# Output of attention in two half sums on 64x32 tiles, placed as pieces in the two lanes of TensorE

## The chip, the core and the metric

One Trainium2 chip, of which the program uses one core. The metric is the time of one execution of the whole kernel on the device, in microseconds (us). One core has a TensorE (PE, whose weight loads the profile lists apart as PEld), a VectorE (DVE), a ScalarE (ACT), a GpSimd (POOL), a SyncE (SP) that issues most transfers, an on-chip memory of 128 partitions, and eight accumulator banks that TensorE writes.

## What is computed

A diffusion transformer block on 16 samples of 256 tokens by 256 features, with 16 heads of 16 features, all in fp32:

```python
x_norm = modulate(_ln(x), shift_a, scale_a)
q, k, v = jnp.split(x_norm @ W_qkv + b_qkv, 3, axis=-1)
attn_w = softmax(einsum('bhqd,bhkd->bhqk', q, k) * scale)
x = x + gate_a * (einsum('bhqk,bhkd->bhqd', attn_w, v) @ W_proj + b_proj)
k_c, v_c = jnp.split(_ln(context) @ W_kvc + b_kvc, 2, axis=-1)
c_attn_w = softmax(einsum('bhqd,bhsd->bhqs', _ln(x) @ W_qc + b_qc, k_c) * scale)
x = x + einsum('bhqs,bhsd->bhqd', c_attn_w, v_c) @ W_cproj + b_cproj
h = gelu(modulate(_ln(x), shift_m, scale_m) @ W_mlp1 + b_mlp1)
x = x + gate_m * (h @ W_mlp2 + b_mlp2)
```

## The kernel before

**Units and beats.** Each sample has two attentions, self (`s`) and cross (`c`): 32 units, one after the other, then a stage for the MLPs. A unit is eight *beats*, one for each pair of heads. In beat k, TensorE makes the scores of pair k of the current unit, keys by queries (words `t`, into the two banks of the tile `st`), and the scores of the next unit's heads, queries by keys (`s`, into the banks `s0` and `s1`), of which VectorE takes the row maxima (`mx`). ScalarE turns `st` into the weights `pt` with one exp of 128x1024 (word `E`, function `exp`). The tile `st` exists once, so the next beat's `t` waits until that exp has read it. Of `pt` there are five buffers.

**Two lanes.** Nearly all matmuls have a contraction of 64 rows. The lower rows (0 to 63) and the upper rows of the array are two lanes that run at the same time. `PLAN` (L1108) has a row for each beat: words issued before, words of lane x (the lower half), words of lane y (the upper half), and words issued after. The function `beside` writes the two lanes into one program order: it always takes the next matmul from the lane whose cost so far is lower. A matmul of 64 rows by 256 columns costs 1, and a transpose of 64 columns costs 0.53 (`HALF`). `Q12` means twelve matmuls of the query projection of a later unit; K, V and P (output projection) likewise. `T`, `U`, `A0`, `A1`, `a`, `m0`, `m1` are transposes by halves (`half_turns`): each half of the array writes its own half of one bank, and the later half first waits (`after`) until the earlier one is complete. All engines execute in the order of the program.

**Output of attention.** `av_part(u, g)` sums weights times values for four heads over all 128 key rows: weights loaded 128x32, so that four heads stand in four strips of 32 columns of the array, and a second pass over the other 128 keys. The words `o0` and `o1` run two such calls each, 16 matmuls in one block that uses the whole array: `o0` behind beat 4 (pairs 0 to 3), `o1` behind beat 0 of the next unit (pairs 4 to 7). fp32 operands take two passes, so the trace has 32 records for these 16 matmuls. ACT then copies the bank (`o`) into `oT`, 128x512. The transposes `A0` and `A1` turn `oT`, `norm` divides by the sums, `a` turns the result back, and P projects it.

**Banks.** Banks 0 and 1 are `st`, 2 and 3 are `s0` and `s1`. The tag `tr` (`SHORT`) has two banks, which the tiles of `T`, `U`, `A0`, `A1`, `a`, `m0`, `m1` and `o` take in turn, and `gen` (`LONG`) two for the projections. A tile that takes a bank waits until the last reader of the tile before has finished.

**Words of ScalarE.** `kh` and `qh` write the high parts of K and Q (two instructions each), `m0s` and `m1s` the negated maxima, `pe` copies the projection (`t_s`, `t_c`), `Te`, `Ue`, `ae` copy transposes (`y_c` or `y_s`, `y_q`, `y_ac`), `Vk` the values (`v`).

Every instruction is issued through one helper, so the profile puts all of them on L51; they are told apart by the names of their tiles.

## Time and profile before

| | |
|---|---|
| time, median of 2 runs | 738.29 us (736.37 to 740.21) |
| profiled execution, its own time | 737.4 us |
| its span, first to last instruction | 735.6 us |
| TensorE busy | 728.9 us (99%) |
| VectorE, ScalarE, GpSimd busy | 584.8, 555.5, 546.3 us |
| blocks of attention output, first to last start | 45.2 to 552.9 us |
| granted TensorE clock | 0.999 |

A row of a timeline reads: start and length in us, engine, line, operation, output tile <- input tiles, shape, count, and in brackets the idle time before it with what ended it. Matmul records are pipelined: each record's length holds the time until its last result is written, so records overlap, and the pace is read from the starts. A row of a group reads: engine, operation, tiles, shapes, count | busy time in us, mean ns of one | idle time before.

### The profile page before, as it was taken

What the parts mean: (1) busy time and instruction counts of PE and PEld (TensorE: products, weight loads), DVE (VectorE), ACT (ScalarE), POOL (GpSimd) and SP (SyncE); (2) the same over time, 40 slices, a digit from 0 to 9 for tenths busy, and PEclk for the clock granted to TensorE, in tenths of its full rate; (3) what the DMA queues carried; (4) which work ended last, traced back from release to release, by engine and by line L of the source; (5) the groups of instructions that cost most, each with busy time, mean ns of one, the idle gap of its engine ahead of it and who ended that gap; (6) DMA issues with size and microseconds to landing.
All of it is one profiled execution on the core that took longest, in us unless ns stands there. A gap on an engine that the chain in (4) does not pass through costs nothing.

```text
span 735.6 us, 25307 instructions
## 1 busy us (share of the span) xinstructions
PE 728.9 (99%) x10112; PEld 644.8 (88%) x10112; DVE 584.8 (79%) x1217; ACT 555.5 (76%) x959; POOL 546.3 (74%) x571
## 2 busy tenths in 40 slices
PE   9999999999999999999999999999999999999997
PEld 9878888888888888888888888888889999999997
DVE  4788898989888888988888989888735577687772
ACT  3268898888888888888888888899887655555553
POOL 6777688869687786968778798788657766767753
PEclk9999999999999999999999999999999999999999
DMA  6754454543545454454545555455312323323331
GB/s 190 205 166 142 125 142 134 141 122 101 155 114 155 125 144 137 107 152 112 160 126 139 143 156 146 126 151 140 96 60 58 102 61 98 98 90 102 87 77 38
DMA packets 94825, 90.60 MB, mean 123 GB/s; under 512 B 9266, under 2 KB 90452, under 8 KB 94708
## 3 DMA queue, kind: packets, MB, share of 16 engines
q1 hardware_dynamic: 94244, 88.20, 42.8%
q8 instruction: 80, 1.31, 0.8%
q0 software_dynamic: 192, 0.52, 0.3%
q14 instruction: 37, 0.30, 0.1%
q10 hardware_dynamic: 272, 0.26, 0.1%
HBM read 26.97 MB, written 8.46 MB: 48 GB/s over the span
## 4 chain that ended last, share of the span: by engine, by line
PE 93%; DVE 3%; POOL 2%; issue 1%; ACT 1%; DMA 1%; SPq 0%; POOLq 0%; ACTq 0%
PE s L51 18%; PE o L51 16%; PE st L51 16%; PE ph L51 10%; PE ps_q L51 5%; PE ps_qc L51 4%; PE ps_v_c L51 3%; PE ps_kc L51 3%; PE ps_P_s L51 3%; PE ps_k L51 2%; PE ps_v_s L51 2%; PE ps_P_c L51 2%; DVE mx L51 1%; PE psT_q L51 1%; PE ps_h L51 1%; PE psA_s L51 1%
## 5 line engine op out<-in xcount | busy, mean ns | idle before, releaser
L51 DVE TENSOR_REDUCE mx<-s 128x2 f32<-128x512 f32 x504 | 324.8, 684 | 64.4 <-PE s L51 57.7
L51 ACT ACTIVATE pt<-st 128x1024 f32<-128x1024 f32 x252 | 258.9, 1027 | 16.4 <-PE st L51 10.4
L51 PE MATMUL s<-big 63*128 63x256 f32 (+1 forms) x1024 | 184.0, 297 | 0.2
L51 PEld LDWEIGHTS s<-big 63*128 63x128 f32 (+1 forms) x1024 | 133.4, 186 | 18.7 <-DVE l_kc L51 6.6
L51 PE MATMUL st<-big 64*128 64x256 f32 (+1 forms) x1024 | 134.6, 298 | 0.5 <-ACT pt L51 0.2
L51 POOL TENSOR_TENSOR hl<-hf,hh 128x512 fp32r<-128x512 f32 x64 | 87.0, 1361 | 52.9 <-ACT hh L51 52.8
L51 PE MATMUL o<-pt,v 128*32 128x256 f32 x2048 | 123.8, 382 | 0.0
L51 PEld LDWEIGHTS st<-big 64*128 64x128 f32 (+1 forms) x1024 | 96.3, 186 | 16.1 <-issue 13.1
L51 PEld LDWEIGHTS o<-pt,v 128*32 128x32 f32 x2048 | 60.1, 110 | 41.4
L51 ACT ACTIVATE hf<-ph,bT 128x256 f32<-128x256 f32 x114 | 47.8, 471 | 33.1 <-PE ph L51 33.0
L51 ACT ACTIVATE hh<-ph,bT 128x256 fp32r<-128x256 f32 x114 | 47.9, 472 | 28.0 <-PE s L51 14.4
L51 ACT COPY oT<-o 128x512 f32<-128x512 f32 x63 | 36.9, 586 | 33.1 <-PE o L51 33.1
L51 PE MATMUL st<-big,hh 128*128 128x256 f32 x256 | 46.7, 282 | 0.0
L51 PE MATMUL s<-big,hh 128*128 128x256 f32 x256 | 46.7, 281 | 0.0
L51 PE MATMUL ph<-wkch,wself 128*128 128x256 f32 x224 | 44.4, 282 | 0.0
L51 PE MATMUL ph<-wqch,wself 128*128 128x256 f32 x224 | 44.3, 282 | 0.0
L51 PE MATMUL ps_k<-xTh_s,wself 64*128 64x256 f32 (+1 forms) x232 | 43.6, 294 | 0.0
L51 POOL TENSOR_SCALAR xn_c<-c,mv_c,rs_c 128x256 f32<-128x256 f32 x32 | 39.0, 1227 | 1.7
L51 PE MATMUL ps_q<-xTh_s,wself 64*128 64x256 f32 (+1 forms) x240 | 39.7, 282 | 0.0
L51 PE MATMUL ps_P_s<-wself,xTh_as 64*128 64x256 f32 x256 | 39.1, 282 | 0.0
L51 PEld LDWEIGHTS s<-big,hh 128*128 128x128 f32 x256 | 39.0, 189 | 0.0
L51 PEld LDWEIGHTS st<-big,hh 128*128 128x128 f32 x256 | 39.0, 189 | 0.0
(250 smaller groups left out, 2500.4 us busy)
## 6 DMA issues: line engine op xcount, KB each, us to landing
big<-h_kc SPq DMA_DIRECT2D x64, 128.0 KB
big<-h_qc SPq DMA_DIRECT2D x64, 128.0 KB
big<-h_k SPq DMA_DIRECT2D x62, 128.0 KB
big<-h_q SPq DMA_DIRECT2D x62, 128.0 KB
big<-l_k SPq DMA_DIRECT2D x32, 128.0 KB
big<-l_q SPq DMA_DIRECT2D x32, 128.0 KB
g<-gd SPq DMA_DIRECT2D x16, 256.0 KB
c<-in_ctx_dram SPq DMA_DIRECT2D x16, 256.0 KB
```

What stands on the lines that cost most here:

```text
L51: i = f(*a, **k)
```

## The change

The sum over 128 key rows is made in two halves of 64 rows. The function `av_halves(u, i)` handles two pairs of heads, 2i and 2i+1, in one bank: half 0 is eight matmuls of 64 rows by 32 columns in the lower half of the array (two blocks of keys times four strips), half 1 eight in the upper half, which add into the same bank and wait for the last matmul of half 0 (`after`). Each half is a word of one lane, `O0` to `O3`, with a cost of 0.91 for a matmul (`OCOST`). `PLAN` now has O0 in beat 3, O1 in beat 5, O2 in beat 7 and O3 in beat 1 of the next unit; the words `o0` and `o1` are gone, and pieces of Q, P and V stand in other beats. `a`, `ae` and `ac` move from beat 5 to beat 4. The copies of `o` become four of 128x256 (`k0` to `k3`, function `av_keep`), each in the words behind its beat. As the heads of a bank are others than before, `norm` writes other columns of `A`, and the rows of W_proj and W_cproj, which are split into high and low parts early on, are loaded a second time in that order by four transfers each (`f_rows`). The last O3 of the program is done whole (`av_all`).

TensorE, from the end of beat 0 of unit 9 (`psm_1` is its `m1`), before: the block `o_2` of unit 8, of which the first four of 16 rows are shown, stands between this beat and the next.

```order
L51 MATMUL st<-big_75 128x256 x2
L51 MATMUL s_111<-big_76 128x256
L51 MATMUL st<-big_75 128x256
L51 MATMUL s_111<-big_76 128x256
L51 MATMUL psm_1_3786<-ident,mx_81 128x64
L51 MATMUL o_2_3808<-pt_4_3618,v_80 32x256
L51 MATMUL o_2_3808<-pt_5_3663,v_80 32x256
L51 MATMUL o_2_3808<-pt_6_3728,v_80 32x256
L51 MATMUL o_2_3808<-pt_7_3773,v_80 32x256
```

The same place in the changed program:

```order
L51 MATMUL s_111<-big_76 128x256
L51 MATMUL st<-big_75 128x256
L51 MATMUL s_111<-big_76 128x256
L51 MATMUL psm_1_4156<-ident,mx_81 128x64
L51 MATMUL s_110<-big_76 128x256
L51 MATMUL st<-big_75 128x256
L51 MATMUL s_110<-big_76 128x256
L51 MATMUL st<-big_75 128x256 x2
L51 MATMUL ps_P_s_4115<-wself,xTh_as_3989 128x256
L51 MATMUL st<-big_75 128x256
L51 MATMUL ps_P_s_4115<-wself,xTh_as_3989 128x256
L51 MATMUL o_3_4192<-pt_6_4078,v_80 32x256
```

Beat 1's `s` and `st` now follow beat 0's directly, and the output of attention comes behind them, one row in turn with the other lane.

TensorE at the start of beat 3 of unit 9 in the changed program (`psT_c` is the word T, `psA_c` A1, `o_0` is O0, whose bank is that of T):

```order
L51 MATMUL psT_c_4251<-ident,xn_c_3891 128x64 x2
L51 MATMUL psA_c_4258<-ident,oT_2_4150 128x64 x4
L51 MATMUL ps_v_s_4275<-wself,xTh_s_3881 128x256 x3
L51 MATMUL s_110<-big_76 128x256
L51 MATMUL ps_q_4210<-xTh_s_3881,wself 128x256
L51 MATMUL s_110<-big_76 128x256
L51 MATMUL ps_q_4210<-xTh_s_3881,wself 128x256
L51 MATMUL o_0_4293<-pt_0_4176,v_78 32x256
L51 MATMUL ps_q_4210<-xTh_s_3881,wself 128x256
L51 MATMUL o_0_4293<-pt_1_4231,v_78 32x256
L51 MATMUL ps_q_4210<-xTh_s_3881,wself 128x256
```

Before, no `o` stood between T and the end of beat 4; now O0 comes a few matmuls behind T.

ScalarE from beat 7 of unit 8 to beat 4 of unit 9, before:

```order
L51 ACTIVATE h_k_3782<-ps_k_3667,bqkv 128x256 x2
L51 ACTIVATE m_1_3799<-psm_1_3786 16x128
L51 ACTIVATE pt_0_3806<-st 128x1024
L51 COPY oT_3_3825<-o_2_3808 128x512
L51 ACTIVATE pt_1_3871<-st 128x1024
L51 COPY t_s_3892<-ps_P_s_3747 128x512
L51 ACTIVATE pt_2_3915<-st 128x1024
L51 COPY y_c_3917<-psT_c_3883 128x512
L51 ACTIVATE pt_3_3949<-st 128x1024
L51 ACTIVATE h_q_3954<-ps_q_3841,bqkv 128x256 x2
L51 ACTIVATE pt_4_3972<-st 128x1024
```

And in the changed program:

```order
L51 COPY oT_2_4150<-o_2_4097 128x256
L51 ACTIVATE h_k_4152<-ps_k_4029,bqkv 128x256 x2
L51 ACTIVATE m_1_4169<-psm_1_4156 16x128
L51 ACTIVATE pt_0_4176<-st 128x1024
L51 ACTIVATE pt_1_4231<-st 128x1024
L51 COPY oT_2_4150<-o_3_4192 128x256
L51 COPY t_s_4268<-ps_P_s_4115 128x512
L51 ACTIVATE pt_2_4279<-st 128x1024
L51 COPY y_c_4281<-psT_c_4251 128x512
L51 ACTIVATE pt_3_4337<-st 128x1024
L51 COPY oT_0_4342<-o_0_4293 128x256
L51 ACTIVATE h_q_4344<-ps_q_4210,bqkv 128x256 x2
```

The copies of `o` now stand ahead of `h_k` and `h_q`, which stand ahead of the exps of beats 0 and 4.

```diff
@@ -255,7 +255,19 @@
 
     def f_split(i):
         w = (Wp, Wkc, Wqc, Wvc, Wcp)[i]
-        split(w[0], w[1], (gA, cB, cB, cB, cB)[i][(3, 2, 3, 4, 1)[i]])
+        if i in (0, 4):
+            f_rows(i // 4)
+        split(w[0], w[1], turned[i] if i in turned else cB[(0, 2, 3, 4)[i]])
+
+    turned = {}
+
+    def f_rows(i):
+        w_ap = (W_proj, W_cproj)[i]
+        t = turned[4 * i] = work.tile([P, KC, H], F32, tag="x1", name=f"wrow{i}", bufs=7)
+        src = w_ap.rearrange("(a k g r) c -> k g a r c", a=2, k=2, g=2)
+        for k in range(KC):
+            for g in range(2):
+                SP.dma_start(t[64 * g:64 * g + 64, k], src[k, g])
 
     wm = []
 
@@ -630,12 +642,11 @@
         def norm(hf):
             if hf == 0:
                 o.A = work.tile([P, NT, H], F32, tag="A", name=f"A_{name}", bufs=1)
-            pv = o.ps.rearrange("p (x h c) -> p x h c", x=4, h=4)
-            rc = work.tile([P, 4, 4, 1], F32, tag="rc", name=f"rc{hf}_{name}")
+            pv = o.ps.rearrange("p (t g c) -> p t g c", t=NT, g=8)
+            rc = work.tile([P, NT, 8, 1], F32, tag="rc", name=f"rc{hf}_{name}")
             DVE.reciprocal(rc, pv[:, :, :, HD:HD + 1])
-            A = o.A.rearrange("p t (r f) -> p (t r) f", r=2)[:, :, 64 * hf:64 * hf + 64]
-            DVE.tensor_tensor(A.rearrange("p x (h i) -> p x h i", h=4),
-                              pv[:, :, :, 0:HD], rc.to_broadcast([P, 4, 4, HD]), ALU.mult)
+            A = o.A[:, :, P * hf:P * hf + P].rearrange("p t (g i) -> p t g i", g=8)
+            DVE.tensor_tensor(A, pv[:, :, :, 0:HD], rc.to_broadcast([P, NT, 8, HD]), ALU.mult)
 
         aT = transposed(lambda: o.A, f"a{name}", pool=True)
 
@@ -766,22 +777,41 @@
             for f in pieces:
                 next(f)
 
-    def av_part(u, g):
-
-        if g % 2 == 0:
-            u.po = ps_gen(f"o_{u.n}_{g}", SHORT).rearrange("p (g n) -> p g n", g=2)
-        for c in range(NT):
-            for h in range(4):
-                par, pair = g % 2, g // 2 * 4 + h
-                PE.matmul(u.po[h * 32:(h + 1) * 32, g % 2], u.v[:, c, par * 8 + pair], u.pt[pair][:, par, c],
-                          start=(c == 0), stop=(c == NT - 1), tile_position=(0, h * 32))
-        if g % 2 == 1:
-            oT = work.tile([P, 2, N], F32, tag="oT", name=f"oT_{u.n}_{g}")
-            last = u.n == nu - 1 and g == 3
-            (DVE.tensor_copy if last else ACT.copy)(oT.rearrange("p g n -> p (g n)"),
-                                                    u.po.rearrange("p g n -> p (g n)"))
-            u.oT.append(oT)
-
+    def av_halves(u, i):
+
+
+        po = ps_gen(f"o_{u.n}_{i}", SHORT)
+        done = []
+
+        def half(hf):
+            rows = slice(64 * hf, 64 * hf + 64)
+            if hf:
+                after(done[0])
+            for c in range(NT):
+                for j in range(4):
+                    par, pair = j // 2, 2 * i + j % 2
+                    ins = PE.matmul(po[32 * j:32 * j + 32, :N], u.v[rows, c, par * 8 + pair], u.pt[pair][rows, par, c],
+                                    start=(hf == c == 0), stop=(hf == 1 and c == NT - 1),
+                                    tile_position=(64 * hf, 32 * j), skip_group_check=True)
+                    if c == NT - 1 and j == 3:
+                        done.append(ins.ins.name)
+                    yield OCOST
+        u.po[i] = po
+        return half(0), half(1)
+
+    def av_keep(u, i):
+        if i % 2 == 0:
+            u.oT.append(work.tile([P, 2, N], F32, tag="oT", name=f"oT_{u.n}_{i}"))
+        last = u.n == nu - 1 and i == 3
+        (DVE.tensor_copy if last else ACT.copy)(u.oT[i // 2][:, i % 2], u.po[i][:, :N])
+
+    def av_all(u, i):
+        for h in av_halves(u, i):
+            for _ in h:
+                pass
+        av_keep(u, i)
+
+    OCOST = 0.91
 
     seq = [("s", b) for b in range(5)]
     for b in range(B):
@@ -794,7 +824,7 @@
         u.n, u.kind, u.b = n, kind, b
         u.qk, u.v = big[n % 3], vts[n % 3]
         u.q, u.k = u.qk[:, 0], u.qk[:, 1]
-        u.oT, u.pt = [], {}
+        u.oT, u.pt, u.po = [], {}, {}
         units.append(u)
     nu = len(units)
 
@@ -1106,14 +1136,14 @@
 
     none = (), ()
     PLAN = [
-        ("kh", "s t m1", "m1 t s", "m1s kH E o1 add gate kl"),
-        ("c1", "s t Q12", "t P2 s P10", "L1 ld kL E"),
-        ("", "s t T pe A1 V3", "s t Q4 T A1 Q1", "hadd E L2 Te Tc c2"),
-        ("", "s t V9", "Q1 t s Q6", "E n1"),
-        ("qh store", "s t", "s t qH", "E L3 o0 ql qL"),
-        ("", "t s a E m0 K6", "t s V4 a m0 V2", "ae ac m0s e5 lc s1"),
-        ("", "s t K1 A0 K5 U E", "V2 t s V4 U A0", "begin e6 Vk Ue s6"),
-        ("", "s t P12", "K2 t s K1 K9", "E n0 Uc s7 e7"),
+        ("kh", "s t m1", "m1 t s", "m1s kH E add gate kl"),
+        ("c1", "s t O3 Q6", "t P2 s P7 O3", "L1 ld kL E k3"),
+        ("", "s t Q6 T pe A1 V3", "s t P3 T A1", "hadd E L2 Te Tc c2"),
+        ("", "s O0 t V9", "Q5 t s Q7 O0", "E n1 k0"),
+        ("qh store", "s t a", "s t V3 qH a", "E L3 ql ae ac qL"),
+        ("", "s O1 t E m0 K6", "t s V4 m0 V2 O1", "m0s k1 e5 lc s1"),
+        ("", "s t A0 K6 U E", "s t V3 U A0", "begin e6 Vk Ue s6"),
+        ("", "s t O2 P12", "K2 t s K1 K9 O2", "E n0 Uc s7 e7 k2"),
     ]
     lanes = {}
 
@@ -1139,15 +1169,10 @@
         c5 = unit(n + 5)
         ln = lambda v, i: lambda *a: v.ln[i].steps
 
-        def attention(v, hf):
-            if v:
-                av_part(v, 2 * hf)
-                av_part(v, 2 * hf + 1)
-
         on = lambda v, f: f if v else lambda: None
         T1 = lx and (lx.T[1],)
         do = {
-            "E": exps, "o1": lambda: attention(prev, 1), "o0": lambda: attention(cur, 0),
+            "E": exps, "k3": on(prev, lambda: av_keep(prev, 3)), **{f"k{i}": lambda i=i: av_keep(cur, i) for i in range(3)},
             "kh": on(q2, lambda: q2.K.high()), "kl": on(q2, lambda: q2.K.low()),
             "kH": on(q2, lambda: q2.K.send_high()), "kL": on(q2, lambda: q2.K.send_low()),
             "qh": on(q2 and hasattr(q2, "Q"), lambda: q2.Q.high()), "ql": on(q2 and hasattr(q2, "Q"), lambda: q2.Q.low()),
@@ -1180,6 +1205,7 @@
             "U": on(lx, lambda: lx.T[1].halves()),
             "A1": on(p1, lambda: p1.halves(1)), "A0": lambda: cur.post.halves(0),
             "a": on(p1, lambda: p1.aT.halves()),
+            "O3": on(prev, lambda: av_halves(prev, 3)), **{f"O{i}": lambda i=i: av_halves(cur, i) for i in range(3)},
         }
         on_x = {"Q": (q2, "Q"), "V": (q2, "V"), "K": (q3, "K"), "P": (None if whole_p else p1, None)}
         on_y = {"Q": (q2, "Q"), "V": (q2, "V"), "K": (q3, "K"), "P": (p2, None)}
@@ -1230,7 +1256,7 @@
     for b in range(2):
         M[b].xT = M[b].src.xT
     done = {
-        "av": lambda: (av_part(last, 2), av_part(last, 3)), "P": lambda: (q.proj(0), q.proj(1)), "PF": q.finish,
+        "av": lambda: av_all(last, 3), "P": lambda: (q.proj(0), q.proj(1)), "PF": q.finish,
         "A1": lambda: o.turn(1), "N1": lambda: o.norm(1), "aT": o.aT.turn, "aL": lambda: (o.aT.high(), o.aT.low_dve()),
         "C": lambda: (o.proj(0), o.proj(1)), "CF": o.finish,
     }
```

## The prediction, made before the result was known

> **What bounds the kernel now.** First the page: its span, the engines, the clock, and the chain that ended last.
>
> ```profile
> span 735.6 us, 25307 instructions
> PE 728.9 (99%) x10112; PEld 644.8 (88%) x10112; DVE 584.8 (79%) x1217; ACT 555.5 (76%) x959; POOL 546.3 (74%) x571
> PEclk9999999999999999999999999999999999999999
> PE 93%; DVE 3%; POOL 2%; issue 1%; ACT 1%; DMA 1%; SPq 0%; POOLq 0%; ACTq 0%
> ```
>
> TensorE carries 93% of the chain at full clock. But a busy PE is not PE at its pace, so next come the starts on TensorE in the timeline around one unit (beat 0 starts at 311.05).
>
> ```profile
> 303.14 0.51 PE L51 MATMUL st<-big 64*128 64x256 f32 x4
> 303.58 1.93 PE L51 MATMUL o<-pt,v 128*32 128x256 f32 x32
> 305.45 0.51 PE L51 MATMUL st<-big 64*128 64x256 f32 x4
> ...
> 310.81 0.28 PE L51 MATMUL ps_P_s<-wself,xTl_as 64*128 64x256 f32 x1
> 310.83 0.28 PE L51 MATMUL ps_k<-xTl_s,wself 64*128 64x256 f32 x1
> 310.93 0.28 PE L51 MATMUL ps_P_s<-wself,xTl_as 64*128 64x256 f32 x1
> 310.95 0.28 PE L51 MATMUL ps_k<-xTl_s,wself 64*128 64x256 f32 x1
> 311.05 0.28 PE L51 MATMUL s<-big 63*128 63x256 f32 x1
> ...
> 311.74 1.94 PE L51 MATMUL o<-pt,v 128*32 128x256 f32 x32
> 313.61 0.39 PE L51 MATMUL st<-big 64*128 64x256 f32 x1
> ...
> 317.29 0.28 PE L51 MATMUL ps_q<-xTh_s,wself 64*128 64x256 f32 x1
> 317.45 0.51 PE L51 MATMUL st<-big 64*128 64x256 f32 x4
> ...
> 319.64 1.94 PE L51 MATMUL o<-pt,v 128*32 128x256 f32 x32
> ```
>
> Both lanes start a matmul every 0.12 us (310.81 to 310.93, 310.83 to 310.95): a step is 0.12. A unit takes 319.64 - 303.58 = 16.06. A block of output lasts 1.87 from its start to the next `st` (303.58 to 305.45). Now ScalarE over the same unit:
>
> ```profile
> 311.27 0.84 ACT L51 ACTIVATE h_k<-ps_k,bqkv 128x256 fp32r<-128x256 f32 x2 [0.54 <-PE ps_k L51]
> 312.13 0.27 ACT L51 ACTIVATE m<-psm 16x128 fp32r<-16x128 f32 x1
> 312.43 1.03 ACT L51 ACTIVATE pt<-st 128x1024 f32<-128x1024 f32 x1
> 313.74 0.59 ACT L51 COPY oT<-o 128x512 f32<-128x512 f32 x1 [0.29 <-PE o L51]
> 314.39 1.02 ACT L51 ACTIVATE pt<-st 128x1024 f32<-128x1024 f32 x1
> 315.88 0.59 ACT L51 COPY t_s<-ps_P_s 128x512 f32<-128x512 f32 x1 [0.47 <-PE ps_P_s L51]
> 316.37 1.03 ACT L51 ACTIVATE pt<-st 128x1024 f32<-128x1024 f32 x1
> 317.28 0.59 ACT L51 COPY y_c<-psT_c 128x512 f32<-128x512 f32 x1
> 318.06 1.02 ACT L51 ACTIVATE pt<-st 128x1024 f32<-128x1024 f32 x1 [0.18 <-PE st L51]
> 318.98 0.83 ACT L51 ACTIVATE h_q<-ps_q,bqkv 128x256 fp32r<-128x256 f32 x2
> 319.81 1.02 ACT L51 ACTIVATE pt<-st 128x1024 f32<-128x1024 f32 x1
> ...
> 324.88 0.58 ACT L51 COPY v<-ps_v_s 128x512 f32<-128x512 f32 x1
> 325.52 0.59 ACT L51 COPY y_q<-psT_q 128x512 f32<-128x512 f32 x1
> ```
>
> The reader is to see a second loop that is nearly as long as TensorE's. `st` starts, 0.6 later the exp (303.14's `st` and 317.45's: 318.06), 1.03 later it ends, and only then may the next `st` start: 1.7 a beat, 8 x 1.7 = 13.6 a unit, without what ScalarE puts in between. In beat 0 the exp starts 1.38 after the beat (312.43 - 311.05), since `h_k` and `m` stand ahead of it, and ends at 313.46. The next `st` starts at 313.61. TensorE doesn't stand still in between, because the block of 311.74 lies exactly there. The block behind beat 4 covers `h_q` and the exp of 319.81 in the same way. **The two blocks are TensorE's work and the cover of the exp loop at once.** That a waiting `st` holds both lanes shows at 317.29 to 317.45: the exp of 316.37 ends at 317.40, and although V and Q steps stand behind `st` in both lanes, nothing starts before it.
>
> **The change, part by part.** First the groups of like instructions that give the length of a single one (count, busy time, mean ns):
>
> ```profile
> L51 PE MATMUL o<-pt,v 128*32 128x256 f32 x2048 | 123.8, 382 | 0.0
> L51 ACT ACTIVATE pt<-st 128x1024 f32<-128x1024 f32 x252 | 258.9, 1027 | 16.4 <-PE st L51 10.4 <-PE s L51 0.2
> L51 ACT COPY oT<-o 128x512 f32<-128x512 f32 x63 | 36.9, 586 | 33.1 <-PE o L51 33.1
> ```
>
> *TensorE's own work.* The block of 1.87, with 0.2 to enter it (`st` of 303.14 has its last start 0.51 - 0.28 later, at 303.37, and `o` starts at 303.58), costs 2 x 2.0 = 4.0 a unit. In its place come four pieces of eight matmuls in each lane. No row shows a 64x32 tile beside a 64x128 one. Bounds: a round of four strips lasts about 0.22 in the block ((1.93 - 0.38) / 7, a record being 0.38), and a matmul takes two passes.
>
> If the four strips of a half run at once, a matmul costs 2 x 0.22 / 4 = 0.11, a half 0.87; if one waits for the other, 0.22 and 1.75. Below 0.11 nothing in the rows leads. I take 0.87, the block's own pace. With 2 steps for `s` and `t` each, 2.1 for a transpose word, 7.3 for an O, the longer lane of each beat has, before, 4.5, 16, 13.2, 13, 4, 12.7, 14.3, 16 = 93.7 steps, and after, 4.5, 20.3, 17.2, 23.3, 9.1, 17.8, 14.2, 23.3 = 129.7. That is 11.2 + 4.0 = 15.2 before and 15.6 after; where a lane that is short in one beat goes ahead in the next, the lanes' mean of 120.8 counts, 14.5. So between -0.7 and +0.4 a unit: TensorE gains little. The waits decide.
>
> *The waits, followed through one unit of the changed program,* in us from the start of beat 0. A copy of 128x256 is taken as 0.37 (1027 at 1024 columns and 586 at 512 give 0.86 ns a column).
>
> 1. O2's upper half ends with beat 7, so its copy starts at 0.2 (before, 0.06 behind the block's end) and `h_k` behind it at 0.6, `m` 1.45, exp 1.75 to 2.8. Beat 0's matmuls end at 0.54. Next on TensorE are `s` and the `st` of beat 1, which waits until 2.9; no block lies there now. O3 is queued behind it.
> 2. Beat 1 goes on from 2.9 with 20.3 steps: 5.3. Three steps of P now lie in beat 2, so `t_s`, at 315.88 early in beat 2, comes 7 steps and the matmul's 0.28 later: 6.4. Exp 6.9 to 7.9, `y_c` until 8.5 (as 315.88, 316.37, 317.28 follow each other).
> 3. Beat 2's 17.2 steps end at 7.4. O0, two steps into beat 3, takes T's bank, which `y_c` has to read first: it waits from 7.6 to 8.6, and Q, `st` and `s` behind it.
> 4. The 21.3 steps left end at 11.1. The copy of O0 (11.3), `h_q` (0.83) and then the exp: 12.5 to 13.6. Beat 4's 9.1 steps end at 12.2. Beat 5's `st` waits until 13.7.
> 5. Beat 5 ends at 13.7 + 2.1 = 15.8. In lane x `st` stands behind O1 now, so its exp runs 15.3 to 16.3, then `m` and the copy of O1 (17.0). A0 reads that: it starts at 17.1, where PE without a wait would be at 16.3.
> 6. Beat 6 ends at 18.2. The exp (17.0 to 18.0), `v` and `y_q` (0.59 each, 324.88 and 325.52) end at 19.1. In a unit with U, O2 takes U's bank and waits from 18.7 to 19.2; 19.3 steps more, 21.5. In one without, 23.3 steps from 18.2, 21.0.
>
> Followed the same way, the program before gives 15.7 against its 16.06, so the method runs 2% short. The difference is 21.5 - 16.1 = 5.4 in 16 units and 21.0 - 16.1 = 4.9 in 14 (the first and last unit lack parts): 155 us.
>
> *Edges.* The block's rows show 0.09 lost on entry (0.21 between starts in place of a step) and 0.1 on leaving (303.58 + 1.93 - 0.38 = 305.13 for the last round, 0.22 for it, then 305.45). Four such edges a unit lie on the path: 4 x 0.1 x 30 = 12; between 0, if the other lane covers them, and 24.
>
> *Four copies for two*: 2 x (2 x 0.37 - 0.59) = 0.3 more of ScalarE a unit, inside the chain above. Then the loads, for which two rows of the early part are nearest:
>
> ```profile
> 35.44 2.87 DMA x<-in_x_dram
> 43.80 0.61 POOL L51 CAST xTh_s<-y_s 128x512 fp32r<-128x512 f32 x1 [1.35 <-ACT y_s L51]
> ```
>
> *Second weight loads*: the splits on POOL wait for transfers issued just before; the nearest row is a 256 KB load on the chain, bound 0 to 2 x 2.9, taken as 0, since POOL stands 1.35 idle behind the first split.
>
> `norm`, `s`, `mx` and the MLP stage stay. Sum: 737.4 + 155 + 12 = 904 on the profiled execution's own time, which lies 0.9 under the median of the runs: **904 us**.
>
> **Rivals.** *A. Each change of tile shape stops the array.* Then no piece runs beside another: two passes of 0.22, an edge of 0.1, a step of 0.12, an edge of 0.1, 0.76 for what costs 0.12. 64 pieces a unit x 0.64 x 30 = 1230: about 1970 us. For it: the edges are the same 0.2 and 0.3 at both blocks. Against it: there the shapes overlap in rows, which these lanes don't. The Trainium skill, page "TensorEngine Tiling (Array Packing)", section "Tiling Modes", under "Key Properties", says that changing the tiling mode, not only the tile, drains TensorE; the edges agree with it, and no run so far shows whether it holds across two halves.
>
> *B. The two passes of a piece hold back the next matmul*, so that a half costs 1.75. The longer lane has four halves on the path, 4 x 0.88 = 3.5, up to 6.4 if the other lane is held to 0.22 a step too; 5 x 30 = 150: 1055 us. Against it: 16 matmuls of two passes in 1.93. [...]
>
> One more view, the busy times of the unit from 311.05 (TensorE, its weight loads, VectorE, ScalarE, GpSimd, then the clock):
>
> ```profile
> 311.05:327.22 16.17, 16.17 (x273) 13.79 (x270) 13.61 (x28) 13.78 (x21) 9.21 (x11) 1.00 0.56 160
> ```
>
> *C. A wait in one lane doesn't hold the other* (not slower). Then lanes fill each other's gaps, the unit is bound by the lanes' 14.5 (ScalarE has 13.8 busy in a unit), and 30 x 1.6 less gives 690 us. It decides from the point where the waits a unit fall under 16.1 - 14.5 = 1.6; the chain has 5.4. Against it stands 317.45.
>
> That the pieces don't stand beside other work is excluded by the program's order.
>
> **How the numbers follow.** Chances: the forecast 0.69 (of itself 810 to 980: only the waits of points 1 and 3 at the low end, edges and transfers in full and 5% of a unit more at the high end), A 0.12, B 0.11, C 0.08. The range takes in the forecast and B and leaves out A and C: 800 to 1070. About 2%, or 15 us, is what a measurement of this kernel can tell from no change. C gives faster 0.06 and, where its waits half remain, same 0.02; the rest, 0.92, is slower.
>
> **What would show it.** PE's busy share falls from 99% to 80-90%, and its idle time stands ahead of `st` (released by the exp), of `o` (released by `y_c`, `y_s`, `y_q`) and of `psA` (released by the copy of `o`). Each unit, read from exp to exp, takes about 21 us, of which 2.3 lie between beat 0 and beat 1. Rounds of four `o` records still start 0.22 apart while the other lane steps at 0.12; under A no two shapes overlap, under B a step beside `o` takes 0.22. The MLP stage after the last unit stays as long. The prediction is wrong if TensorE stays as full as before, or if single pieces, not waits, take the time.

## The result, and the profile after

| | before | changed |
|---|---|---|
| time, median of 2 runs | 738.29 us (736.37 to 740.21) | 3408.8 us (3406.01 to 3411.58) |
| span of the profiled execution | 735.6 us | 3404.2 us |
| TensorE busy | 99% | 99% |
| granted TensorE clock, mean | 0.999 | 0.545 |
| one unit, from exp to exp | 16.1 us | 96 to 103 us |
| first to last piece or block of output | 45.2 to 552.9 us | 43.3 to 3220.2 us |

The changed kernel takes 4.62 times as long (95% interval 4.60 to 4.63). The MLP stage behind the last output is as long as before (3404.2 - 3220.2 = 184 us, 735.6 - 552.9 = 183 us), so all of it lies in the units. The page of the changed kernel, from its top:

```profile
span 3404.2 us, 29419 instructions
PE 3368.5 (99%) x12160; PEld 1488.6 (44%) x12160; DVE 599.1 (18%) x1217; ACT 573.1 (17%) x1023; POOL 544.2 (16%) x571
PEclk7555555555555555555555555555555555555599
PE 97%; ACT 2%; DVE 0%; issue 0%; DMA 0%; POOL 0%; SPq 0%; ACTq 0%; POOLq 0%
L51 PE MATMUL o<-pt,v 64*32 64x256 f32 x4096 | 1895.6, 620 | 1.8 <-ACT y_q L51 1.0
```

TensorE is as busy as before and carries even more of the chain; the forecast's 80 to 90% with idle gaps is not there. What changed shows in other rows. The weight loads fell from 88% to 44% of a span 4.6 times as long, so the matmuls stand far apart; and the clock is at half from the second of 40 slices until the MLP stage. The first piece shows how it begins (TensorE in the timeline of the changed kernel, then its windows: length, busy time of TensorE, of its weight loads, VectorE, ScalarE and GpSimd, clock, DMA share, GB/s):

```profile
43.28 0.62 PE L51 MATMUL o<-pt,v 64*32 64x256 f32 x2
43.83 0.38 PE L51 MATMUL ps_q<-xTh_s,wself 64*128 64x256 f32 x1
44.14 0.62 PE L51 MATMUL o<-pt,v 64*32 64x256 f32 x2
...
48.05 1.06 PE L51 MATMUL o<-pt,v 64*32 64x256 f32 x2
49.04 0.58 PE L51 MATMUL s<-big 63*128 63x256 f32 x1
49.54 1.06 PE L51 MATMUL o<-pt,v 64*32 64x256 f32 x2
```

```profile
44.00:46.00 2.00, 2.00 (x8) 0.78 (x9) 0.08 (x1) 0.00 (x0) 0.00 (x0) 1.00 0.17 44
46.00:48.00 2.00, 2.00 (x6) 0.60 (x4) 0.00 (x0) 0.00 (x0) 0.00 (x0) 0.72 0.63 183
48.00:50.00 2.00, 2.00 (x6) 0.64 (x5) 0.00 (x0) 0.00 (x0) 0.00 (x0) 0.50 0.67 223
```

The reader is to see three things. A piece (two records, one for each pass) and a step of the other lane no longer overlap: the step starts 0.55 behind the piece and the next piece 0.31 behind the step, a pair every 0.86 us (43.28 to 44.14). Both lanes together made two steps in 0.12 before. And some 3.5 us after the first pair the clock falls to half, and a pair takes 1.49 (48.05 to 49.54). That is the forecast's rival A with a second cost on top of it.

### The profile page after: what moved, and what is told of

The parts are those of the page before. It is cut to its first block, busy times and chain, and to the rows that moved or that the text cites. A ratio compares the mean times of both kernels' runs of the same rounds, so it can differ in the third digit from the quotient of the medians.

```text
span 3404.2 us, 29419 instructions
## 1 busy us (share of the span) xinstructions
PE 3368.5 (99%) x12160; PEld 1488.6 (44%) x12160; DVE 599.1 (18%) x1217; ACT 573.1 (17%) x1023; POOL 544.2 (16%) x571
## 4 chain that ended last, share of the span: by engine, by line
PE 97%; ACT 2%; DVE 0%; issue 0%; DMA 0%; POOL 0%; SPq 0%; ACTq 0%; POOLq 0%
PE o L51 52%; PE s L51 8%; PE st L51 6%; PE ps_kc L51 4%; PE ps_P_s L51 3%; PE ps_k L51 3%; PE ps_P_c L51 3%; PE ps_qc L51 3%; PE ps_v_c L51 3%; PE ps_q L51 3%; PE ps_v_s L51 2%; PE ph L51 2%; PE ps_h L51 2%; ACT pt L51 1%; PE psA_c L51 1%; PE psm L51 1%
## 5 line engine op out<-in xcount | busy, mean ns | idle before, releaser
L51 PE MATMUL o<-pt,v 64*32 64x256 f32 x4096 | 1895.6, 620 | 1.8 <-ACT y_q L51 1.0
L51 PEld LDWEIGHTS o<-pt,v 64*32 64x32 f32 x4096 | 320.9, 134 | 397.9 <-issue 353.1
L51 PE MATMUL s<-big 63*128 63x256 f32 (+1 forms) x1024 | 373.9, 502 | 7.8 <-DVE mx L51 7.5
L51 PEld LDWEIGHTS s<-big 63*128 63x128 f32 (+1 forms) x1024 | 217.6, 292 | 314.2 <-issue 226.3
L51 PE MATMUL st<-big 64*128 64x256 f32 (+1 forms) x1024 | 260.5, 442 | 20.8 <-ACT pt L51 20.8
L51 PEld LDWEIGHTS st<-big 64*128 64x128 f32 (+1 forms) x1024 | 188.1, 315 | 87.2 <-issue 51.0
L51 PE MATMUL ps_k<-xTh_s,wself 64*128 64x256 f32 (+1 forms) x232 | 117.2, 535 | 0.0
L51 PE MATMUL ps_P_s<-wself,xTh_as 64*128 64x256 f32 x256 | 116.0, 515 | 0.0
L51 PE MATMUL ps_v_s<-wself,xTh_s 64*128 64x256 f32 x224 | 82.5, 467 | 0.0
L51 PE MATMUL ps_kc<-xTh_c,wkch 64*128 64x256 f32 x128 | 70.8, 553 | 0.0
```

The lines of the kernel that those rows point to most:

```text
L51: i = f(*a, **k)
```

## The experiments

Each run is listed with its label; the kernel before, run on the same chips, took 737.2 to 737.3 us. "Clock" is the mean granted clock, and "a unit" the time from exp to exp: the mean of 24 units in the middle, or the values that occur. The runs with 64x128 and 64x64 pieces, with four or eight together and with O0 alone are single runs; for the others the table has the median of four, and of two for the changed kernel.

| kernel | us | clock | a unit |
|---|---|---|---|
| before with the second weight loads (`rows_only`) | 750.3 | 0.993 | 16.2 |
| halves as blocks at the old places (`halves_old`) | 811.0 | 0.985 | 17.7 |
| four whole blocks behind beats 0, 2, 4, 6 (`blocks_even`) | 840.5 | 0.987 | 18.1 or 19.2 |
| four whole blocks behind beats 1, 3, 5, 7 (`blocks4`) | 912.5 | 0.976 | 20.8 or 22.3 |
| pieces of 64x128 in one pass (`wide128_r`) | 938.8 | 0.957 | 21.9 |
| pieces 64x32, eight together (`halves8`) | 1356.4 | 0.772 | 28 to 46 |
| only O0 as pieces (`one_piece`) | 1462.1 | 0.756 | 38.8 |
| pieces of 64x128, two passes (`wide128`) | 1604.3 | 0.940 | 42.7 |
| pieces 64x32, four together (`rounds4`) | 1619.4 | 0.657 | 43.5 |
| changed kernel | 3408.8 | 0.545 | 100.8 |
| pieces of 64x64 (`wide64`) | 3513.6 | 0.554 | 103.9 |

**The shape of the tile (`wide128`, `wide64`).** Only the columns of a piece's tile change; places, order and passes stay.

```diff
-  ins = PE.matmul(po[32 * j:32 * j + 32, :N], u.v[rows, c, par * 8 + pair], ..., tile_position=(64 * hf, 32 * j))
+  h0 = min(par * 8 + pair, 12)                                                            # wide128
+  ins = PE.matmul(po[:, :N], u.v[rows, c, h0:h0 + 4], ..., tile_position=(64 * hf, 0))
+  h0 = min(par * 8 + pair, 14)                                                            # wide64
+  ins = PE.matmul(po[64 * (j // 2):64 * (j // 2) + 64, :N], u.v[rows, c, h0:h0 + 2], ..., tile_position=(64 * hf, 64 * (j // 2)))
```

> The pieces stay in their places and in their order, one in turn with the other lane, and keep their two passes, but each loads 128 columns of weights instead of 32 (four neighbouring heads), so its tile is 64x128 like its neighbours'. The sums of attention come out mixed; that part of the computation is left wrong. Theory D (each change of tile shape empties the array, in both halves): no shape changes are left, so the loss goes. A piece costs two steps in its lane, 2 x 0.12, the longer lanes have some 165 steps a unit, 19.8 us, and the waits of the prediction come on top: 850 to 1010 us at full clock. Theory F (the two fp32 passes of a piece hold up the other lane, whatever the shape): a pair of piece and step still takes 0.85 us or more, and the time stays above 2000 us.

> As the run with 64x128 pieces, but each piece loads 64 columns of weights (two neighbouring heads), so its tile is 64x64, neither that of its neighbours nor that of the change; the sums of attention are mixed. Theory D1 (any tile shape other than the neighbours' empties the array): a pair of piece and step takes the changed kernel's 0.85 us at full clock and 1.49 at half: 3300 to 3500 us. Theory D2 (only the narrow 32-column tile does it): as with 64x128, a pair 0.43, about 1600 us.

Measured: 1604.3 us at clock 0.940, and 3513.6 us at 0.554. TensorE in the timeline, first with 64x128, then with 64x64 pieces:

```profile
703.74 0.59 PE L51 MATMUL o<-pt,v 64*128 64x256 f32 x2
703.96 0.38 PE L51 MATMUL ps_q<-xTh_s,wself 64*128 64x256 f32 x1
704.17 0.59 PE L51 MATMUL o<-pt,v 64*128 64x256 f32 x2
```

```profile
1500.20 1.11 PE L51 MATMUL o<-pt,v 64*64 64x256 f32 x2
1501.24 0.58 PE L51 MATMUL s<-big 63*128 63x256 f32 x1
1501.74 1.11 PE L51 MATMUL o<-pt,v 64*64 64x256 f32 x2
```

With one shape in both lanes a pair takes 0.43 (703.74 to 704.17) instead of 0.86, and the clock stays near full. With 64x64 it takes 1.54 at half clock, as with 64x32. So it is the change of shape, with 64 columns as with 32, that empties the array, and D1 holds. The Trainium skill, page "TensorEngine Tiling (Array Packing)", section "Tiling Modes", says under "Key Properties" that changing the tiling mode drains TensorE; the trace agrees, and shows that this holds when the other shape is in the other half of the array (0.86 a pair against 0.43). But D's time for 64x128 was wrong, 1604 for 850 to 1010, and F's above 2000 too. A cost was left that neither had.

**The two passes (`wide128_r`).** The same 64x128 pieces, with operands in a type that takes one pass.

```diff
-  vts = [const.tile([P, NT, NH, 32], F32, name=f"v{i}") for i in range(3)]
+  vts = [const.tile([P, NT, NH, 32], F32R, name=f"v{i}") for i in range(3)]
-  u.pt[pair] = work.tile([P, 2, NT, N], F32, tag="pt", ...)
+  u.pt[pair] = work.tile([P, 2, NT, N], F32R, tag="pt", ...)
```

> The run with 64x128 pieces again, same order, but weights and values of attention are kept in the rounded type of the other lane matmuls (fp32r), so a piece takes one pass. The sums of attention are mixed as there, and rounded. Theory O (what made that run 1604 us in place of 850 to 1010 is that nothing in the program order overtakes a piece of two passes of 0.216 us, so a pair of piece and step takes 0.43): a piece is now a step like others, 0.12; the unit is what the waits make it, 20 to 22 us as with the four blocks (20.8), with the clock near full: 870 to 950 us. Rival (the pieces collide with the other lane for another reason, such as the bank or the order of their rows): 1300 us or more.

Measured: 938.8 us, clock 0.957. Its timeline in beat 7 of a unit:

```profile
488.73 0.28 PE L51 MATMUL o<-pt,v 64*128 64x256 f32 x1
488.73 0.28 PE L51 MATMUL ps_kc<-xTh_c,wkch 64*128 64x256 f32 x1
488.84 0.28 PE L51 MATMUL o<-pt,v 64*128 64x256 f32 x1
```

Now a pair takes 0.11 and both lanes run at their step. With two passes, the row at 703.74 holds two records that start 0.22 apart (0.59 - 0.38), and the other lane starts one step in each 0.43, with every second record. In the program, piece and step alternate, and a lane gets only a little ahead of that order. How far, the rows just ahead of 703.74 show (the run with two-pass pieces, at the start of beat 3, where up to 703.42 only one-pass matmuls stand; in the program there stand three `ps_v_s`, then `s`, then the first `ps_q`, as in the front part's third order listing):

```profile
702.26 0.36 PE L51 MATMUL ps_v_s<-wself,xTh_s 64*128 64x256 f32 x1
702.29 0.38 PE L51 MATMUL ps_q<-xTh_s,wself 64*128 64x256 f32 x1
702.46 0.27 PE L51 MATMUL ps_v_s<-wself,xTh_s 64*128 64x256 f32 x1
702.58 0.28 PE L51 MATMUL ps_v_s<-wself,xTh_s 64*128 64x256 f32 x1
702.70 0.40 PE L51 MATMUL s<-big 63*128 63x256 f32 x2
703.42 0.48 PE L51 MATMUL o<-pt,v 64*128 64x256 f32 x1 [0.33 <-ACT y_c L51]
703.43 0.50 PE L51 MATMUL ps_q<-xTh_s,wself 64*128 64x256 f32 x2
```

`ps_q` starts ahead of two `ps_v_s` and the `s`, three matmuls that stand before it. Beside pieces of two passes the lead is one piece. Then the faster lane goes at the pace of the slower one, and a piece gives it one step in 0.43, 3.6 steps' time, where `OCOST` reckons 0.91. Theory O's forecast came out, 870 to 950 us. But the run halves the passes and shortens each, 0.22 to 0.11, so a piece also holds its own lane for a quarter of the time; how the 1604.3 - 938.8 = 665 us divide between that and the order, no run separates. The clock has a small share: as an estimate, 0.060 x 1604 - 0.043 x 939 = 56 us, if time goes with the clock.

**The number of changes (`rounds4`, `halves8`).** The same matmuls in the same words, but four or eight behind each other before the other lane has its turn.

```diff
                     if c == NT - 1 and j == 3:
                         done.append(ins.ins.name)
-                    yield OCOST
+                yield 4 * OCOST          # rounds4
+            yield 8 * OCOST              # halves8
```

> The four strips of a round of a piece stand behind each other in the program, and then the other lane has its turn for four matmuls: 16 groups of four a unit in place of 64 single pieces, the matmuls being the same. Theory D: the changes of shape fall to a quarter. A group costs 0.54 (as one piece does, since the four strips run at once), the way back 0.31 and three more steps 0.36: 1.2, 16 of them 19.4, with 7.5 for what is left of the lanes 27 us a unit, about 1070 us if the clock stays full, about 1850 if it falls to half. Theory S (a 64x32 matmul is slow by itself beside other work, wherever it stands): 64 pieces cost what they did, 3000 to 3500 us.

> The eight matmuls of a half of a piece stand behind each other: eight groups a unit. Theory D: a group costs 0.54 + 0.43 for its second round, 0.31 back and six steps more: 2.0, eight of them 16, with 7.5 for the rest 24 us a unit and 1 to 2 of waits: 980 to 1040 us at full clock, up to 1800 at half. Theory S: 3000 to 3500 us. If time goes with the number of shape changes, this run and the one with groups of four lie on one line with the changed kernel, per change and at the same clock.

Measured: 1619.4 and 1356.4 us. TensorE in the timelines, four together, then eight together:

```profile
808.37 1.08 PE L51 MATMUL o<-pt,v 64*32 64x256 f32 x8
809.38 1.22 PE L51 MATMUL ps_v_s<-wself,xTl_s 64*128 64x256 f32 x4
```

```profile
703.56 1.93 PE L51 MATMUL o<-pt,v 64*32 64x256 f32 x16
```

Four pieces together take 1.01 until the next step, one alone 0.99 (48.05 to 49.04), both at half clock: the four strips do run at once, and what costs is the change. Counted in the records, TensorE changes between output and other work 3648 times in the changed kernel, 1012 times with groups of four and 508 times with groups of eight. 3408.8 - 1619.4 over 2636 changes is 0.68 us a change, 1619.4 - 1356.4 over 504 is 0.52; the clock is not the same in the three (0.545, 0.657, 0.772), so they do not lie on one line exactly. Both times lie between theory D's for full and for half clock, and theory S is out.

**The clock (`one_piece`).** O0 stays in pieces in beat 3, and the other three become blocks.

```diff
-  ("c1", "s t O3 Q6", "t P2 s P7 O3", "L1 ld kL E k3"),
+  ("c1", "s t Q6", "t P2 s P7", "L1 ld kL E b3 k3"),
...
-  ("", "s t O2 P12", "K2 t s K1 K9 O2", "E n0 Uc s7 e7 k2"),
+  ("", "s t P12", "K2 t s K1 K9", "E n0 Uc s7 e7 b2 k2"),
```

> Of the four outputs only O0 stands as pieces in the lanes, in beat 3; the others are blocks of 128x32 behind beats 5, 7 and 1 (as in the run with four blocks, 912 us, 20.8 a unit). Theory D: 16 pairs take 16 x 0.855 = 13.7 at full clock and 23.9 at half, in place of a block of 1.0 and 1.0 of steps: 32 to 43 a unit, 1260 to 1570 us. For the clock: if it follows what the array has done in the last few us, it falls a few us after beat 3 has begun and is full again in the other beats, mean 0.7 to 0.85, about 1400 us; if it stays down once it has fallen, mean 0.5 to 0.6 and above 1600 us.

Measured: 1462.1 us, clock 0.756, inside theory D's range and by the first of the two cases for the clock. Windows of 4 us over one unit; in the timeline the pieces stand from 704.94 to 721.8, 0.86 apart at first and 1.49 later:

```profile
704.00:708.00 4.00, 3.68 (x18) 1.50 (x16) 0.69 (x1) 0.89 (x2) 1.88 (x2) 1.00 0.06 20
708.00:712.00 4.00, 4.00 (x11) 1.38 (x10) 0.00 (x0) 0.00 (x0) 0.00 (x0) 0.69 0.00 0
712.00:716.00 4.00, 4.00 (x20) 2.15 (x19) 1.28 (x3) 1.02 (x1) 0.00 (x0) 0.50 0.00 0
...
724.00:728.00 4.00, 4.00 (x44) 3.12 (x43) 2.65 (x6) 2.14 (x5) 1.89 (x2) 0.68 0.70 191
728.00:732.00 4.00, 4.00 (x69) 3.71 (x71) 3.36 (x8) 3.15 (x5) 2.04 (x4) 1.00 0.51 137
```

The clock falls 4 to 5 us after the pieces begin and is back 4 to 6 us after they end, while TensorE's busy time is 4.00 of 4.00 in all of these windows but the first. So it does not follow how busy the row says TensorE is; that it follows how much the array has done fits, but no run varies that alone. The Trainium skill, "TensorE: Matmul & The Clock Gate", Part 1, tells of a monitor with a free-running window of some 3.4 us that switches between full and half clock; the delays agree with one or two such windows, and 0.69 and 0.68 are windows in which it switched. A change of shape is not needed for a fall: with two-pass 64x128 pieces (`wide128`) the clock also stands at half after a wait of 1.14 for the exp at 733.46, and stays there until about 750 with no shape change beside it:

```profile
738.00:742.00 4.00, 4.00 (x18) 3.16 (x17) 0.00 (x0) 0.00 (x0) 0.00 (x0) 0.50 0.03 9
```

**The placement (`blocks4`).** The change without its tiles: heads, norm, copies, and the places of Q, P, V and `a` as in the change, but `b0` to `b3`, blocks of eight 128x32 matmuls over all 128 rows, stand ahead of `k0` to `k3`.

```diff
+  def av_block(u, i):
+      po = u.po[i] = ps_gen(f"o_{u.n}_{i}", SHORT)
+      for c in range(NT):
+          for j in range(4):
+              par, pair = j // 2, 2 * i + j % 2
+              PE.matmul(po[32 * j:32 * j + 32, :N], u.v[:, c, par * 8 + pair], u.pt[pair][:, par, c], ..., tile_position=(0, 32 * j))
-  ("", "s O0 t V9", "Q5 t s Q7 O0", "E n1 k0"),
+  ("", "s t V9", "Q5 t s Q7", "E n1 b0 k0"),
...
```

> The heads of a bank, the norm, the copies and the places of Q, P and V are those of the change, but the output of attention is four blocks of eight 128x32 matmuls over all 128 rows behind beats 3, 5, 7 and 1, none beside other work. So this is the placement of the change without its tiles. The prediction's waits (beat 1's scores waiting for the exp behind k2, h_k and m; beat 5's waiting for the exp behind k0 and h_q) should show here: 11.2 of steps and 4 x 1.1 of blocks are 15.6 a unit, with 2.3 and 1.5 of waits and up to 1 for T's bank 19.5 to 20.5: 840 to 870 us. If the waits are absorbed, 15.6 a unit: 725 to 745 us.

Measured: 912.5 us, 1.238 times the kernel before (1.236 to 1.240). ScalarE and then TensorE around beat 0 of a unit, which starts at 388.60:

```profile
388.74 0.37 ACT L51 COPY oT<-o 128x256 f32<-128x256 f32 x1 [1.47 <-PE o L51]
389.00 0.84 ACT L51 ACTIVATE h_kc<-ps_kc,bT 128x256 fp32r<-128x256 f32 x2
389.87 0.27 ACT L51 ACTIVATE m<-psm 16x128 fp32r<-16x128 f32 x1
390.17 1.02 ACT L51 ACTIVATE pt<-st 128x1024 f32<-128x1024 f32 x1
```

```profile
388.60 0.38 PE L51 MATMUL s<-big 63*128 63x256 f32 x1
...
389.88 0.38 PE L51 MATMUL s<-big 63*128 63x256 f32 x1 [0.48 <-DVE mx L51]
391.24 0.38 PE L51 MATMUL st<-big 64*128 64x256 f32 x1 [0.98 <-ACT pt L51]
```

This is the prediction's point 1, 2.64 from the start of beat 0 to the next `st` where it had 2.9. In this kernel 20.8 us a unit stand against its 21.0, and 912.5 us against its 904. The expectation of this run, 840 to 870, counted fewer waits and was short. The agreement of the totals with the forecast is in part luck: TensorE has no wait here for `y_c`, `y_s` or `y_q`, the bank waits of points 3 and 6 (1.0 and 0.5 a unit there), while four blocks in place of two and a wait of 10.4 us for the second loads are in the time.

**Cover (`blocks_even`).** The same four blocks behind beats 0, 2, 4 and 6, in the rows of the kernel before.

```diff
-  ("kh", "s t m1", "m1 t s", "m1s kH E o1 add gate kl"),
+  ("kh", "s t m1", "m1 t s", "m1s kH E b3 k3 add gate kl"),
-  ("qh store", "s t", "s t qH", "E L3 o0 ql qL"),
+  ("qh store", "s t", "s t qH", "E L3 b1 k1 ql qL"),
```

(In the same way `b0 k0` ends the words behind beat 2, and `b2 k2` those behind beat 6.)

> The four blocks of 128x32 again, but behind beats 0, 2, 4 and 6, in the rows of the kernel before. Theory W (the placement costs because nothing covers the exp of beats 0 and 4, which h_k and h_q hold up): a block of 1.0 covers half of what the block of 1.9 did, so about 0.9 a beat is lost twice, and two more blocks cost two entries and exits, 0.4: 18.3 a unit, 780 to 820 us against the 912 of the blocks behind beats 1, 3, 5 and 7. Rival (it is the copies, the banks and the order of P and Q that cost): 20 a unit or more, 870 to 920 us, or, if four blocks cost only their edges, 745 to 760 us.

Measured: 840.5 us, 1.140 times (1.139 to 1.142). A unit takes 18.1 where T and U do not stand in the way, as W's 18.3 said, and 19.2 where O2 waits for U's bank; the time is above W's 780 to 820. The waits of TensorE (total us, times, longest), first one row of the run with the blocks behind beats 1, 3, 5, 7, then two of this one:

```profile
PE st L51 <- ACT pt L51: 46.9, 62, 1.5
...
PE st L51 <- ACT pt L51: 14.8, 61, 0.4
PE o L51 <- ACT y_q L51: 12.0, 16, 0.8
```

With the blocks moved by a beat, the wait of `st` for the exp falls from 46.9 us in all to 14.8, and the time by 72 us. That speaks for the cover, but the places of Q, P, V and `a` differ between the two runs as well, so how much of the 72 us is the cover's is not shown. The bank waits of points 3 and 6 are there as well (12.0 over 16 units is 0.75 for U, where point 6 had 0.5). Two long waits for POOL, 10.4 us (`ps_k`) and 8.7 us (`ps_P_s`), stand once each, near the start, and are the next experiment's.

**The second loads (`rows_only`).** The kernel before with four more transfers for each of W_proj and W_cproj, rows in the old order.

```diff
+        if i in (0, 4):
+            f_rows(i // 4)
-        split(w[0], w[1], (gA, cB, cB, cB, cB)[i][(3, 2, 3, 4, 1)[i]])
+        split(w[0], w[1], turned[i] if i in turned else cB[(0, 2, 3, 4)[i]])
...
+        src = w_ap.rearrange("(k g p) c -> k g p c", k=2, g=2)
```

> The kernel before, unchanged but for the second loads of W_proj and W_cproj: four transfers each, issued where the change issues them, ahead of their splits (the rows in the old order, so that nothing else changes). The trace of the run with the halves in blocks shows POOL waiting 14.0 and 12.5 us for these transfers, and TensorE 8.8 and 9.0 for what POOL makes behind them. Theory L (the loads cost on the path by themselves): 752 to 765 us. Rival, the prediction's value (hidden, 0): 735 to 742 us.

Measured: 750.3 us, 1.020 times (1.017 to 1.023), just under theory L's 752 and well above the rival's 742. The first four transfers on SyncE and the split that waits for them, then the waits of GpSimd and of TensorE that the kernel before does not have:

```profile
46.30 2.46 SPq L51 DMA_DIRECT2D wrow<-in_L_xcond_W_proj_dram  x4
50.54 0.61 POOL L51 CAST wself<-wrow 128x512 fp32r<-128x512 f32 x1 [10.06 <-DMA wrow<-in_L_xcond_W_proj_dram]
```

```profile
POOL wself L51 <- DMA wrow<-in_L_xcond_W_proj_dram: 10.1, 1, 10.1
POOL wcph L51 <- DMA wrow<-in_L_xcond_W_cproj_dram: 7.5, 1, 7.5
```

```profile
PE ps_k L51 <- POOL xTh_s L51: 5.3, 1, 5.3
PE ps_P_s L51 <- POOL xTh_as L51: 4.5, 1, 4.5
```

POOL's wait begins at 40.48 (50.54 - 10.06). Of its 10.1 us, 5.8 pass before SyncE issues the first of the four transfers, 2.5 while it issues them and 1.8 behind that. The splits stand on POOL ahead of `xTh_s` and `xTh_as`, and POOL works in the program's order; 5.3 + 4.5 of the 13 us are TensorE's wait for these two. The clock, at 0.52 from 51 to 58 us and 0.57 from 78 to 82, right behind these waits, is the likely rest: an estimate, 7 x 0.48 + 4 x 0.43 = 5 us at most.

**The tiles without the mixing (`halves_old`).** All 64x32 matmuls of two outputs as one block at each old place, the lower half of the array on one bank and the upper on the other, then changed over.

```diff
+  def lane(hf):
+      for turn in range(2):
+          m = (hf + turn) % 2
+          if turn:
+              after(done[m])
+          ...                    # eight matmuls of half hf into bank ps[m]
+  beside([lane(0)], [lane(1)])
```

> The same 64x32 matmuls in the same number, but taken out of the lanes: O0 and O1 as one block behind beat 4, O2 and O3 behind beat 0, with the rows of beats as in the kernel before. In a block the lower half of the array makes half 0 of one bank while the upper half makes half 1 of the other, then they change over. Shapes change four times a unit instead of 128. Theory D: the tiles themselves cost nothing; a block is 4 rounds of two passes a lane, 1.73, with a changeover of 0.3 between: 740 to 770 us, and the clock stays full. Theory S (64x32 tiles are slow by themselves, or two halves don't run at once): a block is 3.5 or more, 3.3 more a unit, 840 us or more.

Measured: 811.0 us, 1.100 times (1.097 to 1.103), clock 0.985. A block behind beat 0 with what follows it on TensorE and ScalarE's `m` beside it, then a block behind beat 4:

```profile
393.13 3.02 PE L51 MATMUL o<-pt,v 64*32 64x256 f32 x64
396.08 0.38 PE L51 MATMUL s<-big 63*128 63x256 f32 x1
393.52 0.27 ACT L51 ACTIVATE m<-psm 16x128 fp32r<-16x128 f32 x1
...
313.82 2.35 PE L51 MATMUL o<-pt,v 64*32 64x256 f32 x64
```

The block behind beat 0 takes 2.95 instead of 1.87, the one behind beat 4 2.27 (the next `st` starts at 316.09). If the two halves of the array took turns, its 64 records in four strips would be 16 rounds of 0.22, 3.5 us; so the halves run at once, and the tiles are not slow in their own company. Beyond 8 rounds of 0.22, the trace has 0.27 at the changeover (0.49 between starts in place of 0.22) and an edge in every block. Behind beat 0, a stop of 0.47 follows the first matmul's two passes: the block takes two banks, one of which holds `psm`, and its next start is at 393.84, where `m` has read it (393.52 + 0.27). The expected 740 to 770 left out this wait and the second loads, which cost more here (TensorE waits 9.0 and 8.8 us for POOL).

No kernel here beat the one before.

## Why the prediction was wrong

The direction was right, the size was not: 904 us forecast, 800 to 1070 given, 3408.8 measured.

- **TensorE's own work** is the step that failed. It bounded a half between 0.87 and 1.75, 0.11 to 0.22 a matmul, from the block, in which all matmuls have one shape. Beside the other lane a matmul of a piece takes 0.86 with its step at full clock and 1.49 at half, so a half of eight that alternate takes 6.9 to 11.9 us with its steps (8 x 0.86, 8 x 1.49), where 0.87 was taken. Both bounds were rows of one shape, and the sentence that no row shows two shapes side by side should have moved the upper one: the rows of the block's edges were the only ones with two shapes, and they belong in this term.
- **Edges**: "four such edges a unit" supposed that inside a beat the lanes run beside each other. There are 3648 over 32 units, 114 a unit. In the forecast's own sense, beyond passes and step, two edges cost 0.86 - 2 x 0.22 - 0.12 = 0.30, so one is 0.15 where 0.1 was taken. Against the same-shape pair of 0.43, in which piece and step overlap, a change costs 0.21.
- **Rival A** was what happened, at a chance of 0.12. The reason given against it, that these lanes don't share rows, was an argument without a row. Its price was 1970; with 1.49 in place of 0.76 its own sum gives 64 x 1.37 x 30 = 2630 more, 3370 us. That this comes near 3409 is in part luck: single pieces in turn are 57 a unit (1824 in 32 units), not 64, and the sum leaves out the other steps, which run at half clock too. What A lacked was the clock, which no row of the kernel before shows below 0.99.
- **Rival B** holds too, and was priced too low: the pair without any change of shape is 0.43, not 0.22. Its argument against itself, 16 matmuls in 1.93, did not bear on it: those are in four strips that run at once, and here two lanes alternate. The Trainium skill, "TensorE: Matmul & The Clock Gate", Part 3, has matmuls start and end in strict program order; that does not hold to the letter here (a `ps_q` went ahead of three matmuls at 702.29), but the lead is so short that over a beat it comes to the same.
- **Rival C** is out: in the rows of the two-pass 64x128 pieces, the piece at 703.42 waits for `y_c`, and `ps_q` of the other lane starts only with it, at 703.43. The forecast's own row against C was weak: 317.29 to 317.45 is 0.16 between starts, where a step is 0.12.
- **The waits** (points 1 to 6, 155 us) were right in size, and can be seen only where the tiles are taken out: 750.3 to 912.5 is 162 us, in part by luck, as said at that run. Closest to the change's own places is the run with one-pass pieces: 21.9 us a unit against the forecast's 21.0 to 21.5, and there the bank waits of points 3 and 6 do occur (15.6 us in all for `y_s`, `y_q` and `y_c`). In the changed kernel itself they are nearly gone, 20.8 us for the exp in all, since a unit of 100 us hides them:

```profile
PE st L51 <- ACT pt L51: 20.8, 32, 1.0
```

- **Second weight loads**: taken as 0 inside bounds of 0 and 5.8, they cost 13 us by themselves. The 2.87 of one transfer was the wrong row: POOL waits 10.1 and 7.5, more than half of the first before SyncE issues any of these transfers. In the changed kernel no wait of TensorE for POOL is left among the waits, so there they cost nothing that shows.
- **Signs**: the forecast looked for idle time on TensorE. A busy share of 99% with records that hold their own waiting said nothing either before or after; the starts and the clock did.

Where the 2671 us are, as far as the runs take it apart, each row with one thing more than the row above it (not an exact sum, since waits disappear under what is added):

| step | us | added |
|---|---|---|
| before | 737 | |
| and the second loads | 750 | 13 |
| and the placement, in whole blocks | 912 | 162 |
| pieces in the lanes, one pass, one shape | 939 | 26 |
| two passes in program order | 1604 | 665 |
| two shapes, and with them the half clock | 3409 | 1805 |

The last row was not split by a run. An estimate: 3648 changes are 1824 pairs; 1824 x (0.86 - 0.43) is 780 us at full clock, and 1824 x (1.49 - 0.86) is 1150 for the clock, 1930 together against 1805, while the waits for the exp fall from 60 us to 21 at the same time. What sets the point at which the clock falls stays open; groups of eight change shape 508 times and their clock still falls to 0.56 in some stretches.

## What to carry to other kernels

Before work is put beside other work on TensorE, compare tile shapes: in these runs two halves of the array ran side by side only while both used the same shape, and each change cost 0.15 to 0.21 us at full clock, more than a step of 0.12, so matmuls of another shape belong in few long blocks. In two lanes written into one program order, a matmul's cost must be the time that it holds its own lane (0.43 us for two passes, not its share of the array), since the other lane gets only a few matmuls ahead. A block that looks like pure TensorE work may also be the cover of another engine's chain; take it away and the wait behind it comes out; here the whole placement, waits included, cost 162 us.

## What the runs showed of the hardware that was not expected

- Tiles of 64x32 or 64x64 in one half of the array and 64x128 in the other did not run at once: a pair of 64x32 and 64x128 takes 0.86 us at full clock, of 64x128 twice 0.43 (two passes) or 0.11 (one pass). A 64x64 tile is no better than 64x32 (1.54 and 1.49 a pair at half clock).
- The clock went to half while the profile had TensorE 99% busy: it fell about 4 us after alternating pieces began and came back within 6 us of their end. It fell also in a run without shape changes, to 0.50 behind a wait for the exp.
- In two lanes of one shape, a matmul may start ahead of up to three that stand before it in the program, if these are in the other half of the array; beside two-pass pieces the lead is one piece.
- Four strips of 64x32 together take as long as one (1.01 and 0.99 us until the next step, at half clock).
- Four transfers, 256 KB together, kept POOL waiting 10.1 us, of which 5.8 passed before SyncE issued the first; a single one of 256 KB on the chain took 2.87.
